# A transformer block on one core: score maxima planned up to three units ahead, their high parts from a second reduction, and the inverse steps in a new order

## The chip, the cores and the metric

The kernel runs on one core of a Trainium2 chip. The metric is the device time of one execution in microseconds; of several runs the median counts.

## The reference

A transformer block with conditioning. Two sequences of 2048 tokens, 512 wide, 16 heads of 32, all in float32:

```python
mod = silu(condition) @ Wada + bada
sh_a, sc_a, gt_a, sh_m, sc_m, gt_m = split(mod, 6, axis=1)
xm = layernorm(x, g1, be1) * (1 + sc_a) + sh_a
q, k, v = heads(xm @ Wqkv)
attn = softmax(where(causal, q @ k.T * 32**-0.5, -inf))
x = x + gt_a * ((attn @ v) @ Wproj + bproj)
xm = layernorm(x, g2, be2) * (1 + sc_m) + sh_m
x = x + gt_m * (gelu(xm @ W1 + b1) @ W2 + b2)
```

## The kernel before

The two sequences (`b`, called sequence 0 and 1 here; the class `Row` holds one) go one after the other through QKV, attention and projection; the MLP comes at the end for both. Attention is cut into 16 **units** per sequence, each a group of four heads (`c`, 0 to 3) and a block of 512 queries (`i`, 0 to 3). The order is i = 0, 1, 2, 3 for c = 0 and 0, 2, 1, 3 after it, so units 0, 4, 8, 12 have i = 0 and units 3, 7, 11, 15 have i = 3.

A query's exponentials need its maximum first, and the kernel gets the maxima by computing the scores twice:

- **The scores for the maxima**, queries on the partitions: one matmul into an `s` bank of PSUM (two banks; one in each step borrows an `st` bank) for each head, 128 queries and up to 512 keys (`bank`, L422). VectorE reduces each to one column of `mx`: L441, or L436 with the causal mask on the diagonal. When a unit is complete, `split` (L444) takes the maximum over the key blocks (L453, where there are several), writes it rounded to the matmul's fp32r type as the high part (L455) and the difference as the low part (L456), both into one of the `mhl` tiles. `rows` (L492) transposes that tile on TensorE (tile `ps_m`, in an `s` bank) and spreads it into `fold` on VectorE (L500).
- **The scores for the output**, keys on the partitions: a unit has 4i + 3 **steps**, one for each block of 128 keys with the last two of the diagonal put together. A step (`scores_t`, L524) starts with four `st<-fold` matmuls that put minus the maximum into the four `st` banks; then four heads' score matmuls add to them; ScalarE takes the exponential (L565, tile `e`); GpSimd zeroes what lies above the diagonal (L571). Two steps later TensorE multiplies with the values (tile `o`). For the sums of the exponentials (tile `sm`), GpSimd adds pairs and fours of steps first (L593, tile `ee`).

TensorE's matmuls stand in the order of the program, so the maxima's matmuls are put between those of the steps. A **planner** says how many: `due` (L645) finds the rate of VectorE work, in costs of `width + 190` or `width + 250`, that every later unit needs to be ready; `count` (L460) turns it into a number of scores `n` for this step, but takes none of a unit beyond `u + AHEAD`. `AHEAD` is 2 (L78): in unit 5, maxima of unit 7 may be computed, and none of unit 8. The queries of unit u + 3 are loaded at the start of unit u (L655) into one of AHEAD + 2 = 4 `qst` buffers; the keys of the next c at the start of its predecessor's first unit.

The sums of a unit go to DRAM (L619). Their **inverses** come back later: `load_sums` (L318) reads them spread over the partitions, `invert` (L328) takes the reciprocal on VectorE and stores it, `widen` (L332) copies it 32 times within DRAM, so that the projection can read it beside its operand. `inverses` (L341) places these by unit and step: the sums of units 0 to 11 in unit 12, step 2, their reciprocal in unit 13, step 0, their twelve widenings in pairs in steps 1 to 6 of unit 13; the sums of units 12, 13, 14 each in the next unit (step 6 of unit 13, step 2 of units 14 and 15), the reciprocal two steps later, the widening one after that. All these DMAs, the loads of queries and keys and the stores of outputs are issued from SP's one queue, in the order in which the builder of the program puts them. VectorE, too, works in order: what stands behind a waiting instruction waits.

Of the kernel before, what the change touches and what calls it, by code (L numbers as in the profile page):

```python
# [8 lines left out]
F32 = mybir.dt.float32  # L9
F32R = mybir.dt.float32r  # L10
BF16 = mybir.dt.bfloat16
AF = mybir.ActivationFunctionType
ALU = mybir.AluOpType
AX = mybir.AxisListType
# [3 lines left out]
P = 128  # L18
# [3 lines left out]
QB = 512  # L22
# [5 lines left out]
def dit_block_kernel(  # L28
# [35 lines left out]
    nc = tc.nc  # L64
# [5 lines left out]
    HC = P // HD  # L70
    TQ = QB // P
    NQ = T // QB
# [2 lines left out]
    LAG = 2  # L75
    E_BUFS = 12
    EE_BUFS = 12
    AHEAD = 2  # L78

    const = ctx.enter_context(tc.tile_pool(name="const", bufs=1))  # L80
    dram = ctx.enter_context(tc.tile_pool(name="scratch", bufs=1, space=DRAM))
# [1 line left out]
    def pool(name, bufs=1, **kw):  # L83
# [5 lines left out]
    bp = bp_cm.__enter__()  # L89
# [19 lines left out]
        axis=AX.XY,  # L109
        op=ALU.add,  # L110
# [7 lines left out]
    for n in range(AHEAD + 1):  # L118
        m = bp.tile([P, HC, HD], F32R, tag=f"mhl{n}", name=f"mhl{n}")
# [40 lines left out]
    n_early = (C - 1) * NQ  # L160
# [99 lines left out]
    units = []  # L260
# [4 lines left out]
    last_order = [i for _, i in units[-NQ:]]  # L265
# [8 lines left out]
    class Row:  # L274
# [30 lines left out]

        def load_queries(self, u):
            c, i = units[u]
            t = bp.tile([P, HC, QB], F32R, tag="qst", name="qst", bufs=AHEAD + 2)
            for r in range(4):
                nc.sync.dma_start(  # L310
                    t[r * HD : (r + 1) * HD].bitcast(F32),
                    qd[self.b][c][r // 2, :, i * QB : (i + 1) * QB].rearrange(
                        "(h d) t -> d h t", d=HD
                    ),
                )
            self.qst[u] = t

        def load_sums(self, u0, u1):  # L318

            w = (u1 - u0) * HC * QB // P  # L320
            self.r = bp.tile([P, n_early * HC * QB // P], F32, tag="r", name="r")[:, :w]
            nc.sync.dma_start(self.r, self.flat(sums_d, u0, u1))

        def flat(self, d, u0, u1):
# [15 lines left out]

        def inverses(self, u, n):  # L341

            if u < n_early:
                return
            if u == n_early:
                if n == 2:
                    self.load_sums(0, n_early)
                return
            if u == n_early + 1:
                if n == 0:  # L350
                    self.invert(0, n_early)
                elif n < 7:
                    for k in (2 * n - 2, 2 * n - 1):
                        self.widen(k)
                n -= 4
            if n == 2:
                self.load_sums(u - 1, u)
            elif n == 4:
                self.invert(u - 1, u)
            elif n == 5:  # L360
                self.widen(u - 1)

        def old_queries(self):

            t = bp.tile([P, HC, QB], F32R, tag="qst", name="qst", bufs=AHEAD + 2)
            return t.bitcast(F32)

        def prefetch(self):
# [75 lines left out]
        def split(self, u, mx):  # L444
            nb = units[u][1] + 1
            hl = mhl[u % (AHEAD + 1)][:, :, : 2 * TQ].rearrange(
                "p h (t l) -> p h t l", l=2
            )
            if nb == 1:
                m = mx[:, :, 0]  # L450
            else:
                m = bp.tile([P, HC * TQ], F32, tag="m1", name="m1", bufs=2)
                nc.vector.tensor_reduce(m, mx, axis=AX.X, op=ALU.max)  # L453
            m = m.rearrange("p (h t) -> p h t", h=HC)
            nc.vector.tensor_copy(hl[:, :, :, 0], m)  # L455
            nc.vector.tensor_tensor(  # L456
                hl[:, :, :, 1], m, hl[:, :, :, 0].bitcast(F32), ALU.subtract
            )
# [56 lines left out]
    def attention_phase(row):  # L515
        b, vv, kst, qst = row.b, row.vv, row.kst, row.qst
        with pool(f"att{b}") as ap, pool(
# [121 lines left out]
            for u, (c, i) in enumerate(units):  # L639
                for n, tiles in enumerate(steps_of[u]):  # L640
                    w = sum(QB - q for _, q in tiles)
# [3 lines left out]
            def due(u, step):  # L645

                rate, past = 0.0, weight[step]
                for v in range(u + 1, len(units)):

                    left = sum(weight[step : max(step + 1, starts[v] - 3)])  # L650
                    rate = max(rate, (cum[v] - row.spent) / left)
                return row.spent + rate * past

            for u, (c, i) in enumerate(units):
                if u + AHEAD + 1 < len(units) and u + AHEAD + 1 >= NQ:  # L655
                    row.load_queries(u + AHEAD + 1)
                if u % NQ == 0 and c + 1 < C:
                    row.load_keys(c + 1, 0, NG)
                steps = len(steps_of[u])
                for n_step, tiles in enumerate(steps_of[u]):  # L660
                    last = n_step == steps - 1
                    if n_step == 0:
                        summed, later = set(), []
                        o = ps_op.tile([P, QB], F32, tag="o", name="o")
                        sm = ps_op.tile([P, QB], F32, tag="sm", name="sm")
                    ready = row.at
                    n = row.count(
                        due(u, starts[u] + n_step) - QB // 2, u + AHEAD
                    )
                    es, rest = scores_t(u, n_step, n)  # L670
                    rest = len(row.todo) - rest
                    make_rows = False
                    if u + 1 < len(units) and row.rows_made == u + 1:
                        if last:
                            row.score(row.count(cum[-1], u + 1))
                        make_rows = last or (ready > u + 1 and n_step >= 1)
                    row.inverses(u, n_step)
                    if u == len(units) - 1:
                        row.prepare(n_step)
                    flush(now)  # L680
                    if make_rows:
                        row.rows(u + 1)
                    row.score(max(0, len(row.todo) - rest))

                    def tile_by_tile(dst, lhs, es, tiles, first, last):
                        at = 0
                        for n, (j, q) in enumerate(tiles):
                            products(
                                dst, lambda h: lhs(j, h), es, q, at,
                                first and n == 0, last and n == len(tiles) - 1,  # L690
                            )
                            at += QB - q

                    def values(es=es, tiles=tiles, c=c, o=o, first=n_step == 0, last=last):
                        tile_by_tile(
                            o,
                            lambda j, h: vv[:, j, (c * HC + h) * HD : (c * HC + h + 1) * HD],
                            es, tiles, first, last,
                        )

                    def row_sums(es, last, tiles=((0, 0),), sm=sm, summed=summed):
                        first = not summed
                        summed.add(len(summed))
                        tile_by_tile(sm, lambda j, h: ones[:, :HD], es, tiles, first, last)

                    if later:
                        four_sums(u, *later.pop(0))

                    pending.append((now + LAG, values))
                    if n_step >= i * TQ:  # L710
                        pending.append(
                            (
                                now + LAG,
                                lambda f=row_sums, es=es, tiles=tiles, last=last: f(
                                    es, last, tiles
                                ),
                            )
                        )
                    elif n_step % 2 == 0:
                        even = es  # L720
                    else:
                        ee = pair_sums(u, even, es)
                        if n_step % 4 == 1:
                            ee0 = ee
                        else:

                            end = n_step + 1 == i * TQ
                            for heads in ([(0, 1), (2, 3)] if end else [range(HC)]):
                                later.append((ee0, ee, heads))
                            pending.append(  # L730
                                (
                                    now + LAG + 2 + end,
                                    lambda f=row_sums, ee=ee0: f(ee, False),
                                )
                            )
                    if last:
                        pending.append((now + LAG, lambda u=u, o=o, sm=sm: finish(u, o, sm)))
                    pending.sort(key=lambda p: p[0])
                    now += 1
# [241 lines left out]
    row = Row(0)  # L981
# [492 lines left out]
```

## Time and profile before

| | |
|---|---|
| median of 3 runs | 2513.37 us (2510.52 to 2516.57) |
| the profiled execution | 2510.99 us, its span 2509.3 us, mean granted clock 0.99 |
| TensorE busy | 2440.3 us (97%) |
| VectorE busy | 1401.8 us (56%) |
| ScalarE busy | 892.6 us (36%) |
| GpSimd busy | 978.7 us (39%) |

The profile is one execution. Busy shares are means over phases that differ: the attention of sequence 0 lies at about 230 to 815 us, that of sequence 1 at 1062 to 1636 us, the MLP from 1699 us on. TensorE's busy time counts its pipelined matmuls with ends that are modelled, so that a stall of some tenths of a microsecond doesn't show in it; the spacing of the starts shows it. In a line of the trace, `tile<-tiles` names what is written and read, and the name after the arrow in brackets or behind a bar is what ended the idle time before it.

### The profile page before, as it was taken

Reading aid. Unit: us, or ns where it says so; the run is one execution under the profiler, and the core shown is the slowest. Engines: PE = TensorE matmul, PEld = TensorE weight load, DVE = VectorE, ACT = ScalarE, POOL = GpSimd, SP = SyncE. Lnnn points to the kernel's source line nnn. Section 1 sums busy time; section 2 is a strip of 40 time slices with the busy share of each in tenths; the row PEclk is TensorE's granted clock in tenths of the full one; section 3 lists DMA queues with packets and bytes.
Section 4 is the critical chain, followed back from the end, with each engine's and each line's share of the span. In section 5 each row is a group of like instructions: output and inputs, shape, how many; then the busy total and the mean of one; then the engine's idle time right before and its main releaser. Section 6 shows DMA issues by size and latency. Waiting matters only on the chain.

```text
span 2509.3 us, 30950 instructions
## 1 busy us (share of the span) xinstructions
PE 2440.3 (97%) x10977; PEld 1178.9 (47%) x10977; DVE 1401.8 (56%) x2820; ACT 892.6 (36%) x1667; POOL 978.7 (39%) x1158
## 2 busy tenths in 40 slices
PE   7999999999999999999999999999999999999998
PEld 3445545445444444554554454444444444444443
DVE  3455667767666535567676766664363353344424
ACT  1213555554545012155545454613313312311310
POOL 0052786766762361068667675332101101200200
PEclk9999999999999999999999999999999999999999
DMA  6667123051224695440514113263224233332423
GB/s 223 202 218 202 46 50 87 22 110 43 87 88 144 215 302 193 133 95 22 110 43 110 27 51 118 69 226 114 88 92 140 78 101 109 109 96 70 140 84 96
DMA packets 133445, 285.71 MB, mean 114 GB/s; under 512 B 13301, under 2 KB 42525, under 8 KB 128426
## 3 DMA queue, kind: packets, MB, share of 16 engines
q1 hardware_dynamic: 126226, 257.47, 34.4%
q0 software_dynamic: 5376, 23.07, 2.6%
q10 hardware_dynamic: 1688, 3.19, 0.4%
q8 instruction: 86, 1.41, 0.2%
q14 instruction: 69, 0.57, 0.1%
HBM read 209.76 MB, written 81.79 MB: 116 GB/s over the span
## 4 chain that ended last, share of the span: by engine, by line
PE 62%; DVE 3%; DMA 1%; SPq 1%; issue 1%; ACT 0%; DVEq 0%; ACTq 0%
PE ps_h L192 15%; PE ps_y L192 15%; PE st L192 9%; PE o L192 5%; PE s L192 5%; PE ps_qk L192 4%; PE ps_o L192 3%; PE sm L192 2%; PE ps_v L192 2%; SPq L336 1%; PE ps_xt L200 1%; PE ps_o L200 0%; DMA r<-sum 0%; DMA q<-hl 0%; DVE junk L436 0%
## 5 line engine op out<-in xcount | busy, mean ns | idle before, releaser
L565 ACT ACTIVATE e<-st 128x512 f32<-128x512 f32 (+1 forms) x1152 | 572.8, 579 | 516.7 <-PE st L192 458.0
L441 DVE TENSOR_REDUCE mx<-s 128x1 f32<-128x512 f32 x634 | 429.6, 687 | 236.2 <-PE s L192 233.4
L593 POOL TENSOR_TENSOR ee<-e 128x512 f32<-128x512 f32 x336 | 420.2, 1287 | 242.8 <-ACT e L565 242.8
L192 PE MATMUL s<-kst,qst 128*128 128x512 f32 (+3 forms) x1066 | 483.4, 460 | 28.4 <-DVE mx L441 10.4
L192 PE MATMUL st<-qst,kst 128*128 128x512 f32 (+3 forms) x1280 | 405.3, 393 | 0.0
L192 PE MATMUL o<-e,vv 128*32 128x512 f32 (+3 forms) x2560 | 296.5, 545 | 0.0
L192 PEld LDWEIGHTS s<-kst,qst 128*128 128x128 f32 x1066 | 201.3, 190 | 202.3 <-DVE mx L441 80.4
L192 PE MATMUL ps_h<-sx,w 128*128 128x512 f32 x640 | 286.7, 592 | 0.0
L1245 POOL TENSOR_TENSOR c<-c 128x512 f32<-128x512 f32 x32 | 40.6, 1270 | 626.8 <-DVE c L1207 626.8
L436 DVE CUSTOM_DVE_ANT_0 junk<-s,causal 128x384 bf16<-128x384 f32 (+3 forms) x432 | 212.2, 491 | 126.9 <-PE s L192 118.2
L192 PE MATMUL ps_y<-sh,w 128*128 128x512 f32 x640 | 276.7, 592 | 0.0
L192 PEld LDWEIGHTS st<-qst,kst 128*128 128x128 f32 x1280 | 226.9, 193 | 92.8 <-issue 63.2
L192 PE MATMUL ps_qk<-xmT,wqkv 128*128 128x512 f32 x512 | 242.0, 601 | 2.2 <-DVE xmT L248 2.2
L571 POOL TENSOR_SCALAR_AFFINE_SELECT e<-e 128x128 f32<-128x128 f32 (+1 forms) x384 | 122.8, 344 | 290.2 <-ACT e L565 284.2
L1207 DVE TENSOR_TENSOR h<-c,ps_h 128x512 f32<-128x512 f32 x128 | 88.0, 688 | 232.5 <-PE ps_h L192 232.5
L593 POOL TENSOR_TENSOR ee<-ee 128x512 f32<-128x512 f32 x168 | 211.2, 1285 | 0.0
L192 PEld LDWEIGHTS ps_h<-sx,w 128*128 128x128 f32 x640 | 121.1, 190 | 150.2 <-issue 149.7
L192 PEld LDWEIGHTS ps_y<-sh,w 128*128 128x128 f32 x640 | 120.7, 190 | 147.8 <-issue 146.4
L1231 ACT ACTIVATE h<-h,cols 128x512 f32<-128x512 f32 x128 | 92.3, 721 | 182.4 <-DVE h L1207 182.4
L192 PE MATMUL st<-fold,sel 32*128 32x512 f32 (+1 forms) x1152 | 154.0, 485 | 2.3 <-DVE fold L500 2.0
L192 PEld LDWEIGHTS ps_qk<-xmT,wqkv 128*128 128x128 f32 x512 | 95.2, 192 | 98.7 <-issue 91.2
L192 PEld LDWEIGHTS st<-fold,sel 32*128 32x128 f32 x1152 | 61.2, 183 | 145.3 <-ACT e L565 75.2
(123 smaller groups left out, 2361.8 us busy)
## 6 DMA issues: line engine op xcount, KB each, us to landing
qst<-q SPq DMA_DIRECT2D x128, 256.0 KB
w<-w1d SPq DMA_DIRECT2D x34, 896.0 KB
w<-w2d SPq DMA_DIRECT2D x28, 1024.0 KB
kst<-k SPq DMA_DIRECT2D x24, 1024.0 KB
q<-hl SPq DMA_DIRECT2D x32, 512.0 KB
k<-hl SPq DMA_DIRECT2D x32, 512.0 KB
kst<-k SPq DMA_DIRECT2D x32, 256.0 KB
w<-in_L_cond_W_dram POOLq DMA_DIRECT2D x64, 128.0 KB, 4.3
```

The lines of the kernel that those rows point to most:

```text
L192: return tc.keep_in_program_order(nc.tensor.matmul(*args, **kw))
L200: return tc.keep_in_program_order(nc.tensor.transpose(dst, src, ident[:n, :n]))
L336: nc.sync.dma_start(dst, inv_d[self.b][u].unsqueeze(1).to_broadcast([HC, HD, QB]),)
L436: nc.vector.tensor_tensor_reduce(junk[:, :w], s[:, :w], causal[:, QB - w :], 1.0, MASKED, ALU.add, ALU.max, m,)
L441: nc.vector.tensor_reduce(m, s[:, :w], axis=AX.X, op=ALU.max)
L565: act(nc.scalar.activation(e[:, :w], sts[h][:, :w], AF.Exp))
L571: nc.gpsimd.affine_select(d, d, pattern=[[0, len(tiles)], [1, P]], compare_op=ALU.is_ge, fill=0.0, base=0, channel_multiplier=-1,)
L593: act(engine.tensor_tensor(dst, x, y, ALU.add))
L1207: nc.vector.tensor_tensor(dst, x, y, op)
L1231: nc.scalar.activation(d, d, AF.Gelu, bias=col(r_b1 + chunk, 1))
L1245: nc.gpsimd.tensor_tensor(c1_, c1_, c2_, ALU.subtract)
```

## The change

Three things are changed. `AHEAD` becomes 3, with one exception in steps 0 and 1 of a unit, where the limit stays at u + 2. There is one more `mhl` tile (`AHEAD + 1` of them); the number of `qst` buffers is now `AHEAD + 1`, which is four again, and the queries of the same unit are loaded at the same place. The high part of the maxima is written by a second maximum over the key blocks instead of a copy of the first one's result. And the inverses are placed anew: the first reciprocal in unit 13, step 2, the first twelve widenings one in a step from step 3 of unit 13 on, in the order in which the projection reads them, the other sums loaded in step 3 and inverted and widened in step 6 of the next unit, with a tile of their own (`r1`).

```diff
-    AHEAD = 2
+    AHEAD = 3
...
-            t = bp.tile([P, HC, QB], F32R, tag="qst", name="qst", bufs=AHEAD + 2)
+            t = bp.tile([P, HC, QB], F32R, tag="qst", name="qst", bufs=AHEAD + 1)
...
             w = (u1 - u0) * HC * QB // P
-            self.r = bp.tile([P, n_early * HC * QB // P], F32, tag="r", name="r")[:, :w]
+            tag = "r" if u1 - u0 > 1 else "r1"
+            self.r = bp.tile([P, w], F32, tag=tag, name="r")
...
         def inverses(self, u, n):
-            if u < n_early:
+            k = u - n_early
+            if k < 0:
                 return
-            if u == n_early:
-                if n == 2:
-                    self.load_sums(0, n_early)
-                return
-            if u == n_early + 1:
-                if n == 0:
-                    self.invert(0, n_early)
-                elif n < 7:
-                    for k in (2 * n - 2, 2 * n - 1):
-                        self.widen(k)
-                n -= 4
-            if n == 2:
+            if (k, n) == (0, 2):
+                self.load_sums(0, n_early)
+            elif (k, n) == (1, 2):
+                self.invert(0, n_early)
+                self.early = sorted(
+                    range(n_early), key=lambda v: last_order.index(units[v][1])
+                )
+            elif k and (k > 1 or n > 2) and self.early:
+                self.widen(self.early.pop(0))
+            if k and n == 3:
                 self.load_sums(u - 1, u)
-            elif n == 4:
+            elif k and n == 6:
                 self.invert(u - 1, u)
-            elif n == 5:
                 self.widen(u - 1)
...
             m = m.rearrange("p (h t) -> p h t", h=HC)
-            nc.vector.tensor_copy(hl[:, :, :, 0], m)
+            nc.vector.tensor_reduce(
+                hl[:, :, :, 0],
+                mx.rearrange("p (h t) n -> p h t n", h=HC),
+                axis=AX.X,
+                op=ALU.max,
+            )
...
-                if u + AHEAD + 1 < len(units) and u + AHEAD + 1 >= NQ:
-                    row.load_queries(u + AHEAD + 1)
+                if NQ <= u + AHEAD < len(units):
+                    row.load_queries(u + AHEAD)
...
                     n = row.count(
-                        due(u, starts[u] + n_step) - QB // 2, u + AHEAD
+                        due(u, starts[u] + n_step) - QB // 2, u + AHEAD - (n_step < 2)
                     )
```

More of the change, by code (lines that the diff above doesn't have):

```diff
@@ L341, in inverses @@
         def inverses(self, u, n):
-            if u < n_early:
+            k = u - n_early
+            if k < 0:
                 return
-            if u == n_early:
-                if n == 2:
-                    self.load_sums(0, n_early)
-                return
-            if u == n_early + 1:
-                if n == 0:
-                    self.invert(0, n_early)
-                elif n < 7:
-                    for k in (2 * n - 2, 2 * n - 1):
-                        self.widen(k)
-                n -= 4
-            if n == 2:
+            if (k, n) == (0, 2):
[8 more added lines that the diff above has]
+            if k and n == 3:
                 self.load_sums(u - 1, u)
-            elif n == 4:
+            elif k and n == 6:
                 self.invert(u - 1, u)
-            elif n == 5:
                 self.widen(u - 1)
         def old_queries(self):
-            t = bp.tile([P, HC, QB], F32R, tag="qst", name="qst", bufs=AHEAD + 2)
+            t = bp.tile([P, HC, QB], F32R, tag="qst", name="qst", bufs=AHEAD + 1)
             return t.bitcast(F32)
```

## The prediction

> **What bounds the kernel now.** I read the page first: TensorE is busy in nearly every slice, VectorE in six or seven tenths of the two attention phases (slices 5 to 13 and 17 to 26), so what can be won is TensorE's short stalls there. The dearest VectorE row is the maxima, and its idle time is waiting for TensorE's score matmuls: the two pace each other.
>
> ```profile
> PE   7999999999999999999999999999999999999998
> DVE  3455667767666535567676766664363353344424
> L441 DVE TENSOR_REDUCE mx<-s 128x1 f32<-128x512 f32 x634 | 429.6, 687 | 236.2 <-PE s L192 233.4
> ```
>
> Next, the windows query on tile s over units 3, 4 and 5 of sequence 1, unit 3 cut in two: the stretch, its length, busy time and instructions of TensorE, weight loads and VectorE, clock, DMA.
>
> ```profile
> 1142.75:1181.82 39.07, 13.90 (x36) 6.81 (x36) 21.23 (x36) 1.00 0.12 30
> 1181.82:1197.50 15.68, 0.78 (x2) 0.38 (x2) 1.44 (x3) 1.00 0.03 9
> 1197.50:1213.29 15.79, 5.46 (x14) 2.61 (x14) 8.10 (x14) 1.00 1.03 218
> 1213.29:1259.40 46.11, 18.34 (x48) 8.85 (x48) 28.48 (x48) 1.00 0.34 77
> ```
>
> The score matmuls come unevenly: two in the last five steps of unit 3, then fourteen in the three steps of unit 4. (Where a step has three or more, one goes into an st bank, which this query leaves out.) Stepping L645 to L668 through with the planner's own costs gives exactly the number of score matmuls that the TensorE timeline shows in every one of 144 steps, so I trust it for the changed limit too.
>
> A step runs from its first st<-fold matmul to the next step's. Against it I set a floor: its matmuls at the start-to-start spacing that their kind has where nothing waits (a 512-wide score 0.22 us). What exceeds the floor in sequence 1, by scores in the step:
>
> | scores | steps | excess, us |
> |---|---|---|
> | 0 | 33 | 7.4 |
> | 2, 3 | 5 | 0.6 |
> | 4 | 26 | 7.5 |
> | 5 | 54 | 19.7 |
> | 6 | 23 | 28.1 |
> | 7 | 3 | 3.3 |
>
> Together 66.6 us, and 64.8 in sequence 0. The sixes hold 6.5 in one step that waits for a reciprocal, 13.6 in eight steps that also transpose maxima (1.2 to 2.8 each), 3.4 in one step at half clock, and 0.36 in each of the other thirteen. How such a step stalls (unit 6, step 4):
>
> ```profile
> 1277.60 0.56 DVE L455 CAST mhl<-m 128x16 fp32r<-128x16 f32 x1
> 1278.20 1.19 DVE L456 TENSOR_TENSOR mhl<-m,mhl 128x16 fp32r<-128x16 f32 x1
> ...
> 1279.65 0.49 PE L192 MATMUL s<-kst,qst 128*128 128x512 f32 x1 [1.04 <-DVE mx L436]
> ...
> 1282.52 0.39 PE L192 MATMUL s<-kst,qst 128*128 128x256 f32 x1 [0.41 <-DVE fold L500]
> ```
>
> VectorE is held up in the split, two s banks are full, TensorE waits in order. The reciprocal's stall, unit 13:
>
> ```profile
> 1522.48 20.22 SPq L336 DMA_DIRECT2D wide<-inv  x10
> 1542.75 2.41 SPq L322 DMA_DIRECT2D r<-sum  x1
> ...
> 1553.90 0.25 DVE L329 RECIPROCAL r<-r 128x16 f32<-128x16 f32 x1 [3.69 <-DMA r<-sum]
> ...
> 1554.76 0.80 PE L192 MATMUL s<-kst,qst 128*128 128x512 f32 x1 [3.11 <-DVE mx L441]
> ```
>
> The 8 KB of sums queue behind ten widenings of 256 KB and land 11.1 us after their issue.
>
> **What the Trainium skill says.** "SBUF — State Buffer", Who interferes with whom: a cast can take the port pair that VectorE shares with GpSimd, a tensor_tensor with both inputs in SBUF contends with GpSimd's reads, and a tensor_reduce on this chip never contends. The trace agrees on the kinds: the 24 reductions at L453 take 0.18 to 0.22 us, while the casts reach 7.39.
>
> ```profile
> L455 DVE CAST mhl<-m 128x16 fp32r<-128x16 f32 x24 | 50.9, 2119 | 0.5
> L456 DVE TENSOR_TENSOR mhl<-m,mhl 128x16 fp32r<-128x16 f32 x24 | 13.5, 560 | 0.6
> 1330.62 9.97 POOL L593 TENSOR_TENSOR ee<-e 128x512 f32<-128x512 f32 x8
> 1333.35 7.30 DVE L455 CAST mhl<-m 128x16 fp32r<-128x16 f32 x1
> ```
>
> This cast outlasted six GpSimd additions of 1.29 us, so it isn't just the one in progress that holds it. "DMA: Bandwidth & Descriptors", Queues, rings and completion order: descriptors are consumed in ring order, which fits the 11.1 us. "TensorE: Matmul & The Clock Gate", What's actually happening: after an idle window the clock halves. The window 1550.71 to 1560.85 has a granted clock of 0.66; a stall costs more than itself.
>
> **The change part by part.** *AHEAD 3.* The same units' queries are loaded at the same place (u + 3 before and after) into four buffers as before; only the planner's limit moves, by one unit, from step 2 on. Stepped again, a sequence has 20 steps with no score, 15 with three, 50 with four, 55 with five, 4 with six. TensorE's work is the same; the excess changes. No score: the two opening steps keep 1.6, 18 at 0.15 make 2.7. Three: unit 0's keeps its 2.2, 14 at 0.2 (the only one now shows 0.12) make 2.8. Four: 50 at 0.18 (plain ones now show 0.11 to 0.36) make 9.0. Five: 55 at 0.36 (19.7 over 54) make 19.8. Six: 1.4. Sum 39.5. The transposing steps now hold four or five scores; such ones show an extra 0 to 0.1 now, so 11 give 1.1, and two right behind a split get half of the 2.65 seen, 2.6. That is 43.2.
>
> *Second maximum.* It takes out 32 casts (24 at 2.12, 8 at 0.17: 52 us of VectorE) and adds 32 reductions of about 0.2 (L453's rows), 6.4 us. On the path I count nothing for this alone: the six casts of 7.3 us lie where no scores are planned (TensorE ran on at 2.55 and 3.31 us a step). With AHEAD 3 that cover is gone, four or five scores stand in those steps, and the casts would cost some 5.5 each. The subtraction at L456 stays and still needs the pair. Bounds: 0.2 us when free, 7.3 if it is starved like the cast; its 24 durations reach 1.50, so I take one GpSimd addition at most, and 0.3 us of TensorE for each of 13 splits: 3.9. A sequence is then at 47.1.
>
> *Inverses.* Same eight-kilobyte loads, reciprocals (0.25, the early one 1.34) and stores, same widenings, all on SP. The sums' load now stands behind one widening of unit 13 instead of ten, in a buffer of its own, and the reciprocal comes three steps later, 11 us or more. The 6.5 is therefore in none of my new sums. Behind the reciprocal on VectorE stand the maxima, behind the inverse's store on SP the later widenings; their reader, the projection's operands, comes a unit later. The first reciprocal moves two steps too. A fourth zeroed mhl tile costs 0.17 us before TensorE's first matmul, hidden by the first loads.
>
> Sum: 66.6 + 64.8 − 2 × 47.1 = 37.2. Projection, QKV and MLP phases: nothing. The profiled execution took 2510.99 (span 2509.3), 2.4 under the median 2513.37; so 2474 for such an execution and **2476 us** for the median.
>
> **The rivals.** *Starved subtraction (slower).* At AHEAD 3 the maxima follow each split at once; if GpSimd's additions (busy throughout 1181.82 to 1197.50) keep the subtraction out like the casts, 26 splits cost 7.3 less the 1.8 that two free s banks cover (scores come 0.9 us apart): 26 × 5.5 = 143, hence 2619. It decides from 37 / 26 = 1.4 us a split. Against it: the waits of 1.50 at most, though they always came behind a cast. If only the six at the old places starve, 33 are lost: 2509, no change. *Late queries.* In units 4, 8, 12 scores three ahead start at step 2, two steps of 4.1 us and 1.7 more after their 1 MB was issued (1195.74 in unit 4); at the 204 to 245 GB/s of the windows behind it that takes about 5 us. If they come 3 us too late: 6 × 3 = 18, hence 2494. *Not as it says.* DMA order is the builder's; if the load still lands behind the widenings, 12 us stay: 2488.
>
> **How the numbers follow.** Levelling 0.73, late queries or unmoved load 0.12, six starved or all gains eaten 0.05, starved 0.10. About 0.2%, 5 us, can be told from no change. The likeliest case alone is 2463 to 2490; the range reaches to the six starved, **2462 to 2509**. Faster 0.85, same 0.05, slower 0.10.
>
> **What would show it.** Right: s matmuls in every step of units 3, 7, 11; steps of four at 3.4 to 3.5 us, of five at 3.7 to 3.8; none of 5.8 or 6.1; no wait of L329; reductions at 0.2. Wrong: L456's successor above 2 us, score matmuls waiting for qst's DMA, or TensorE's excess still above 55 us a sequence.

## The result and the profile after

The changed kernel takes **2501.84 us** (median of 6 runs, 2499.7 to 2507.36) against 2515.81 of the kernel before (6 runs, 2510.52 to 2521.73). The medians lie 14 us apart; the ratio given for them is 0.9959 [0.9941, 0.9977], which is 10 us (6 to 15), and the spans of the profiled executions, 2509.3 before and 2499.4 after, lie 9.9 apart. The forecast was 2476. The sign is right and the time lies inside the range, but the gain is between a quarter and two fifths of the 37 us forecast.

The page first. The rows of TensorE and VectorE hardly change, and the dearest VectorE row has the same mean. It counts 28 fewer because as many more of its kind now lie in an `st` bank: more steps have three scores or more.

```profile
PE   7999999999999899999999999999999999999998
DVE  3455766766665635667666776574263353344424
L443 DVE TENSOR_REDUCE mx<-s 128x1 f32<-128x512 f32 x606 | 408.4, 687 | 221.4 <-PE s L192 220.8
```

One slice of TensorE (number 14) has dropped to 8, but it lies at 812 to 875 us, behind the attention of sequence 0, which ends at about 800; in before the same slice is busy for 91% and in after for 90%. It has no part in what follows. Below are the windows on tile `s` of after, at its own borders: unit 3 of sequence 1 cut in two at step 10, then units 4 and 5. The columns are those of the windows shown in the prediction.

```profile
1144.27:1182.58 38.31, 12.69 (x34) 6.39 (x34) 19.77 (x34) 1.00 0.13 31
1182.58:1208.19 25.61, 7.11 (x18) 3.42 (x18) 10.41 (x19) 0.93 0.04 7
1208.19:1221.24 13.05, 3.75 (x9) 1.70 (x9) 5.55 (x9) 1.00 1.00 217
1221.24:1263.36 42.12, 14.81 (x38) 7.14 (x38) 23.19 (x38) 1.00 0.42 95
```

The scores are spread as forecast: 18 `s` matmuls where there were 2, and unit 4 with 9 instead of 14. Unit 4 is shorter by 2.7 us and unit 5 by 4.0. But the last five steps of unit 3 take 25.6 us, 9.9 more than before. Sixteen more scores at 0.22 us are 3.5 us; the rest comes of a wait. The timeline of after shows which, first VectorE and GpSimd, then one line of TensorE (other lines left out):

```profile
1178.74 5.03 POOL L601 TENSOR_TENSOR ee<-ee 128x512 f32<-128x512 f32 x4
1182.79 0.20 DVE L455 TENSOR_REDUCE m<-mx 128x16 f32<-128x48 f32 x1
1182.91 0.19 DVE L458 TENSOR_REDUCE mhl<-mx 128x16 fp32r<-128x48 f32 x1
1183.14 5.57 DVE L464 TENSOR_TENSOR mhl<-m,mhl 128x16 fp32r<-128x16 f32 x1
1183.70 4.97 POOL L601 TENSOR_TENSOR ee<-e 128x512 f32<-128x512 f32 x4
1188.63 0.68 DVE L443 TENSOR_REDUCE mx<-s 128x1 f32<-128x512 f32 x1
...
1189.36 0.48 PE L192 MATMUL s<-kst,qst 128*128 128x256 f32 x1 [4.58 <-DVE mx L443]
```

GpSimd adds without a gap from 1178.74 to 1188.67. Both reductions of the split take 0.2 us. The subtraction (L456 before, L464 now) takes 5.57 us, and it ends at 1188.71, just when that run of additions (L593 before, L601 now) ends. Only then can VectorE reduce the next `s` bank, and TensorE, which had filled both banks and stopped, goes on after 4.58 us. In the window 1187 to 1192 the granted clock is 0.75, so the matmuls behind it pay too: step 10 of the unit takes 9.8 us; before, with two scores, it took 3.0, and in `pool_lo` below, with the same five scores as here, 3.7.

The kinds of the subtraction in after, from the groups by form (busy us, mean ns):

```profile
L464 DVE TENSOR_TENSOR mhl<-m,mhl 128x16 fp32r<-128x16 f32 x24 | 40.4, 1684 | 0.5
L464 DVE TENSOR_TENSOR mhl<-mx,mhl 128x16 fp32r<-128x16 f32 x8 | 9.3, 1165 | 0.2
```

Before, its first form took 13.5 us in all and the cast 50.9. The cast is gone and the subtraction has inherited the wait. The long ones stand in the splits of units 5, 9 and 13, made in units 3, 7 and 11 (5.55, 5.33, 4.17 in sequence 0 and 5.57, 5.30, 4.18 in sequence 1), and in that of unit 3 in sequence 0 (4.97); three of about 2.44 are in splits of units with i = 0. Each of these ten ends within 0.05 us of the end of a run of GpSimd's additions; in the three of 2.44 the run ends with maskings (L579, 0.3 us each). The list of waits names what TensorE waited for, first before, then after (us in all, times, longest):

```profile
PE s L192 <- DVE mx L441: 10.4, 9, 3.2
...
PE s L192 <- DVE mx L443: 24.4, 7, 4.6
...
PE s L192 <- DVE mx L438: 4.2, 2, 4.0
```

The reciprocal of the sums (L329 before, L330 now) no longer waits in unit 13, and that unit takes 41.4 us instead of 52.2, in both sequences.

### The profile page after: what moved, and what is told of

Its sections match the earlier page's. It is cut to its first block, busy times and chain, and to the rows that moved or that the text cites. A ratio compares the mean times of both kernels' runs of the same rounds, so it can differ in the third digit from the quotient of the medians.

```text
span 2499.4 us, 30991 instructions
## 1 busy us (share of the span) xinstructions
PE 2428.3 (97%) x10977; PEld 1178.4 (47%) x10977; DVE 1388.0 (56%) x2821; ACT 894.9 (36%) x1667; POOL 980.3 (39%) x1158
## 4 chain that ended last, share of the span: by engine, by line
PE 62%; DVE 3%; DMA 1%; issue 1%; ACT 0%; SPq 0%; DVEq 0%; ACTq 0%
PE ps_h L192 15%; PE ps_y L192 15%; PE st L192 10%; PE o L192 5%; PE s L192 5%; PE ps_qk L192 4%; PE ps_o L192 3%; PE sm L192 2%; PE ps_v L192 2%; PE ps_xt L200 1%; DVE mhl L464 1%; PE ps_o L200 0%; DMA q<-hl 0%; DVE mx L443 0%; DVE stat L204 0%
## 5 line engine op out<-in xcount | busy, mean ns | idle before, releaser
L443 DVE TENSOR_REDUCE mx<-s 128x1 f32<-128x512 f32 x606 | 408.4, 687 | 221.4 <-PE s L192 220.8
L601 POOL TENSOR_TENSOR ee<-e 128x512 f32<-128x512 f32 x336 | 420.3, 1289 | 242.7 <-ACT e L573 242.7
L192 PE MATMUL s<-kst,qst 128*128 128x512 f32 (+3 forms) x1032 | 469.7, 457 | 29.0 <-DVE mx L443 24.4
L192 PE MATMUL st<-qst,kst 128*128 128x512 f32 (+3 forms) x1280 | 414.4, 391 | 0.0
L438 DVE CUSTOM_DVE_ANT_0 junk<-s,causal 128x512 bf16<-128x512 f32 (+3 forms) x426 | 209.1, 491 | 156.4 <-PE s L192 148.7
L579 POOL TENSOR_SCALAR_AFFINE_SELECT e<-e 128x128 f32<-128x128 f32 (+1 forms) x384 | 123.3, 345 | 283.4 <-ACT e L573 280.7
L601 POOL TENSOR_TENSOR ee<-ee 128x512 f32<-128x512 f32 x168 | 211.5, 1289 | 0.0
```

The costliest lines, as they stand in the source:

```text
L192: return tc.keep_in_program_order(nc.tensor.matmul(*args, **kw))
L438: nc.vector.tensor_tensor_reduce(junk[:, :w], s[:, :w], causal[:, QB - w :], 1.0, MASKED, ALU.add, ALU.max, m,)
L443: nc.vector.tensor_reduce(m, s[:, :w], axis=AX.X, op=ALU.max)
L579: nc.gpsimd.affine_select(d, d, pattern=[[0, len(tiles)], [1, P]], compare_op=ALU.is_ge, fill=0.0, base=0, channel_multiplier=-1,)
L601: act(engine.tensor_tensor(dst, x, y, ALU.add))
```

## The experiments

Two theories were put against each other. **Held subtraction:** the levelling works as forecast, and a subtraction with both inputs in SBUF, waiting for GpSimd, gives most of it back. **Levelling worth little:** the steps of five scores cost what the sixes did, and the waits lie where TensorE would have stood anyway. All times below are medians, and each ratio is to the kernel before, with its 95% interval.

### The subtraction taken away from the contention

`psum_lo`: after, with the first maximum written into an `s` bank of PSUM, so that the subtraction has one input in SBUF. The eight splits with a single key block, which needed no first maximum, get one too.

```diff
-            if nb == 1:
-                m = mx[:, :, 0]
-            else:
-                m = bp.tile([P, HC * TQ], F32, tag="m1", name="m1", bufs=2)
-                nc.vector.tensor_reduce(m, mx, axis=AX.X, op=ALU.max)
+            m = ps_sp.tile([P, QB], F32, tag="s", name="m1")[:, : HC * TQ]
+            nc.vector.tensor_reduce(m, mx, axis=AX.X, op=ALU.max)
```

> The changed kernel, but the maximum m goes to an s bank of PSUM, so that the subtraction has one SBUF input. If the subtraction's waits behind GpSimd's additions ate the levelling (some 49 us over its eight longest places), this lands at about 2450 to 2456 and the subtraction takes under 0.4 us everywhere. If the levelling itself brings no more than the 10 us seen, it stays at 2497 to 2503, with the subtraction short or not.

`pool_lo`: after, with the subtraction on GpSimd.

```diff
-            nc.vector.tensor_tensor(
-                hl[:, :, :, 1], m, hl[:, :, :, 0].bitcast(F32), ALU.subtract
+            act(
+                nc.gpsimd.tensor_tensor(
+                    hl[:, :, :, 1], m, hl[:, :, :, 0].bitcast(F32), ALU.subtract
+                )
             )
```

> The changed kernel with the subtraction on GpSimd, in GpSimd's own order, so that VectorE never waits for the pair. Starved subtraction: 2452 to 2465, a little above the version with m in PSUM, since the transposition that follows a split closely now waits for GpSimd's queue. Levelling without worth: about 2500. GpSimd already the bound: above 2505.

Measured: `psum_lo` **2458.67** (0.9789 [0.9771, 0.9807]), `pool_lo` **2450.26** (0.9756 [0.9737, 0.9774]). Both take away nearly all that was lost, in two different ways. Tile `mhl` in `psum_lo` (ns: least, median, longest) and in `pool_lo`:

```profile
L461 DVE TENSOR_TENSOR mhl<-m,mhl x32: 165/174/178, 117.9 to 1529.6; 128x16 fp32r<-128x16 f32 x32
```

```profile
L465 POOL TENSOR_TENSOR mhl<-m,mhl x24: 216/223/264, 180.2 to 1522.7; 128x16 fp32r<-128x16 f32 x24
```

With one operand in PSUM all 32 take under 0.18 us, beside the same additions on GpSimd. The windows on tile `s` of `pool_lo` for the same stretches of unit 3 (its times are earlier, its work the same):

```profile
1114.69:1152.90 38.21, 12.71 (x34) 6.38 (x34) 19.65 (x34) 1.00 0.12 30
1153.01:1172.25 19.24, 6.64 (x18) 3.32 (x18) 10.43 (x19) 1.00 0.04 10
```

The first ten steps are as in after; the last five take 19.24 us instead of 25.61, at a full clock, which is the 15.7 of before and the 3.5 of the sixteen scores. This is the held subtraction's price in one place. `pool_lo` has no wait of an `s` matmul for VectorE among its eight largest on TensorE; `psum_lo`, whose maximum takes a turn in the two `s` banks, has 13 short ones (5.8 us), which is most of the 8 us between the two.

### Is it the second maximum?

`ahead3_copy`: after, with the copy for the high part, as before.

```diff
-            nc.vector.tensor_reduce(
-                hl[:, :, :, 0],
-                mx.rearrange("p (h t) n -> p h t n", h=HC),
-                axis=AX.X,
-                op=ALU.max,
-            )
+            nc.vector.tensor_copy(hl[:, :, :, 0], m)
```

> The changed kernel with the copy in place of the second maximum: three units ahead and new inverses, casts as before. If either instruction that needs the pair is held through the burst, the cast takes the wait and the subtraction behind it is short: 2495 to 2512, like the changed kernel. If the cast is the worse of the two and the second maximum was what kept it from being slow: above 2520.

Measured: 2500.09 (0.9956 [0.9939, 0.9973]), the same as after. The cast takes the wait again; its groups by form:

```profile
L457 DVE CAST mhl<-m 128x16 fp32r<-128x16 f32 x24 | 35.7, 1488 | 0.7
L457 DVE CAST mhl<-mx 128x16 fp32r<-128x16 f32 x8 | 10.9, 1366 | 0.1
```

The subtraction behind it has a median of 0.18 us and at most 1.22. So of the two instructions, the first takes the long waits, and the second follows free or nearly so. Taking the first out only moves the wait.

`before_reduce`: before, with the second maximum alone (the same edit in the other direction).

> The kernel before with the second maximum alone. If the subtraction takes over the wait of the cast, and the long casts lay under no scores: within 4 us of the kernel before, the subtraction at 4 to 7 us in units 3, 7, 11. If the cast's wait was on the path: 10 us faster or more.

Measured: 2501.71 (0.9952 [0.9933, 0.9971]), 12 us under before (7 to 17). The forecast gave this part nothing. The long waits stay, now in the subtraction (7.2 to 7.7 us), where no scores are planned. The profiled executions show 8.0 us of gain in units 6 and 10, where the wait of cast and subtraction had stood among the steps of six scores: all four take 30.4 us, where three took 31.6 and one 34.6. Of the 34.6, 2.8 us lie in one step at about half clock behind that wait (6.91 us for 4.11), which the other three don't have; so about 5 of the 8.0 come back in all four alike, 1.2 in each. Unit 2 of sequence 1 loses 4.1 us by a subtraction held 4.4; unit 0 of the two sequences gains 2.9, and what remains lies outside the attention, so at most the 8.0 are explained, and the rest of the 12 stays open.

`pool_lo_copyhi`: `pool_lo` with the copy for the high part.

> Three units ahead, new inverses, subtraction on GpSimd, but the high part by the copy on VectorE again. If copy and subtraction are held alike, and the second maximum is worth something only when the subtraction is off VectorE too, the copy is held at the same places for 4 to 6 us and the time is back at 2490 to 2503. If the subtraction alone was the trouble: 2450 to 2458.

Measured: 2459.96 (0.9784 [0.9765, 0.9803]), 10 us above `pool_lo`, and far from the 40 to 50 that a held cast would cost. Its longest cast takes 3.11 us, not 5.7. GpSimd's own subtraction needs the cast's result, and the additions behind it in the program come only after it. Each of the seven casts of over 0.4 us ends within 0.04 us of the end of the last addition in front of it, and the subtraction starts 0.1 us later (for one of 3.11: cast done at 1441.67, subtraction from 1441.75, next addition from 1441.93). The upper expectation left this out.

### The inverses

`before_inv`: before, with the new inverses alone. `pool_lo_oldinv`: `pool_lo` with the old ones. The edit is the hunk of `inverses` and of the tile `r1` in the change's diff, forwards and backwards.

> The kernel before with the new inverses alone. The wait for the sums (about 6.5 us of TensorE in each sequence) goes: 12 to 13 us faster. If the load only lands behind other transfers, or another wait follows: under 4 us.

> The version with the subtraction on GpSimd, with the old inverse steps. If the new inverses are worth what unit 13 showed in the profile of that part alone (5.4 us a sequence), this is 10 to 13 us above that version's 2450: 2460 to 2463. If the wait for the sums was worth only the 3 us that the part alone gained: 2452 to 2455.

Measured: `before_inv` 2507.86 (0.9984 [0.9973, 0.9995]), 4 us under before (1 to 7), where I expected 12. Its profile has unit 13 shorter by 5.4 us in both sequences, as expected, but in that execution the cast of one split in unit 2 was held 4.6 us in both sequences, and that unit was 4 to 5 us longer. `pool_lo_oldinv` 2474.42 (0.9842 [0.9823, 0.9861]), **24 us above** `pool_lo` by the medians and 22 by the ratios, where 10 to 13 were expected. Waits of VectorE, then of TensorE, in it:

```profile
DVE r L329 <- DMA r<-sum: 23.0, 6, 9.2
...
PE s L192 <- DVE mx L441: 16.2, 2, 8.2
```

The same late load that cost one wait of about 4 us a sequence at `AHEAD` 2 costs up to 9.2 at `AHEAD` 3, where the units are shorter and scores stand in every step; unit 13 takes 51.05 and 54.34 us against 41.4.

### The same parts at AHEAD 2

`before_pool`: before, with the second maximum and with the subtraction on GpSimd. `before_pool_inv`: the same with the new inverses. Against `pool_lo`, the second leaves out only `AHEAD` 3, with its fourth `mhl` tile and the exception in steps 0 and 1.

> The kernel before, two units ahead and old inverses, with high parts by the second maximum and the subtraction on GpSimd: VectorE never needs the pair in a split. If the long casts of before lay under no scores, only what stalls in units 2, 6 and 10 can go, 2 to 4 us a sequence: 3 to 9 us faster. If they mattered as they do three units ahead: 30 us faster or more.

> Two units ahead, second maximum, subtraction on GpSimd, new inverses. If the new inverses are worth 5 us a sequence at this limit, the time is 2492 to 2495, and the distance to 2450 (some 43 us) is what three units ahead give when VectorE isn't held. If the part is worth its 3 us here too: about 2500, and three units ahead give 50.

Measured: `before_pool` 2503.66 (0.9959 [0.9944, 0.9975]); `before_pool_inv` 2495.05 (0.9918 [0.9898, 0.9939]). The steps are then: the second maximum and the free splits 10 us (6 to 14), the new inverses 8.6 more (2503.66 to 2495.05), `AHEAD` 3 another 45 (2495.05 to 2450.26). The last two are differences of medians from different series, so good to a few us; by the ratios they are 10 and 41. The levelling is the large part, as forecast; it pays only when nothing holds VectorE at a split: after, which adds `AHEAD` 3 and the new inverses to `before_reduce` and leaves the subtraction on VectorE, takes 2501.84 where that one takes 2501.71.

### How long GpSimd holds it

In after the subtraction waits for the rest of one addition and up to four more of 1.29 us in a row. Two kernels tried to make a gap: `spacer` puts a memset of 128x1 behind each addition on GpSimd, `spacer_wide` a memset of 128x256 behind every second. What the memsets write is not used; everything else is after.

```diff
                 act(engine.tensor_tensor(dst, x, y, ALU.add))
+                if engine is nc.gpsimd and h % 2:
+                    gap = ap.tile([P, 256], F32, tag="gap", name="gap", bufs=2)
+                    act(nc.gpsimd.memset(gap, 0.0))
```

> The changed kernel with a GpSimd memset of one column behind each of its additions; it reads no SBUF, and nothing uses what it writes. If VectorE is kept out as long as GpSimd's reads follow one another and gets the pair in the gap, the subtraction waits 1.4 us at most and the time is 2452 to 2470 (GpSimd has some 50 us more to do). If a gap of this kind gives nothing away, the waits stay at 4 to 6 us and the time at 2495 or above.

> The changed kernel with a GpSimd memset of 256 columns behind every second addition, about 0.3 us that read no SBUF; nothing uses what it writes. If a longer gap in GpSimd's reads lets VectorE in, the subtraction waits 2.7 us at most and the time falls below 2475. If VectorE is held until GpSimd has nothing left to do, the waits stay at 4 us and more and the time at 2490 or above.

Measured: `spacer` 2494.85 (0.9911 [0.9882, 0.9939]), `spacer_wide` **2471.05** (two runs; 0.9828 [0.9803, 0.9853]). The timeline of `spacer` (only GpSimd and the subtraction):

```profile
1323.90 0.12 POOL L604 MEMSET gap<- 128x1 f32 x1
1323.96 1.31 POOL L601 TENSOR_TENSOR ee<-ee 128x512 f32<-128x512 f32 x1
1324.23 6.11 DVE L464 TENSOR_TENSOR mhl<-m,mhl 128x16 fp32r<-128x16 f32 x1
1325.19 0.12 POOL L604 MEMSET gap<- 128x1 f32 x1
1325.25 1.29 POOL L601 TENSOR_TENSOR ee<-e 128x512 f32<-128x512 f32 x1
```

The next addition starts 0.06 us after its memset, before the memset ends, so this was no real gap, and the subtraction was held through five of them, to the end of the run. Its longest holds here are 6.48 us, longer than in after. In tile `mhl` of `spacer_wide`:

```profile
L464 DVE TENSOR_TENSOR mhl<-m,mhl x24: 164/177/2657, 166.9 to 1539.1; 128x16 fp32r<-128x16 f32 x24
L464 DVE TENSOR_TENSOR mhl<-mx,mhl x8: 164/2194/2930, 117.9 to 1405.9; 128x16 fp32r<-128x16 f32 x8
```

Its memsets take 0.31 us, and no subtraction waits longer than 2.93 us, a little over two additions. All nine waits of over 1 us end within 0.05 us of the end of an addition that has a memset behind it. GpSimd has more work than in after (1041.0 us busy against 980.3), and the kernel is 31 us faster. That speaks for the pauses in GpSimd's reads, and against GpSimd's load as such.

## Why the prediction was right and wrong

**Right: the levelling.** Every step has the number of scores that the stepping gave. In `pool_lo`, where no split is held, the plain steps of four (one key block, eight value matmuls, no sums or transposition) take 3.37 to 3.50 us in all 60 cases and those of five 3.64 to 3.93; none of 5.8 or 6.1 is left. In after they are the same except where a held split stands. No score matmul waits for queries. The forecast's excess over the floor, without the splits' 3.9, was 43.2 us a sequence; `pool_lo`, in which the splits are free, has 42.0 and 43.7.

**Wrong: "I take one GpSimd addition at most, and 0.3 us of TensorE for each of 13 splits: 3.9."** This is the step that failed. It rested on 24 durations of the subtraction that reach 1.50 us (1.20 within the attention), all of them behind a cast, which at the six long places had already sat out the run of additions; the text of the rival said so and it was still counted as evidence. The better number stood beside it, the cast's 7.39. What the splits cost is the length of the attention in after less that in `pool_lo`: 570.7 − 539.4 = 31.3 us in sequence 0, 560.4 − 540.8 = 19.6 in sequence 1 (first to last step, from the starts of the `st<-fold` matmuls). That is 50.9 us instead of 7.8, and it matches the spans, 2499.4 − 2448.4 = 51.0. Both of the forecast's own signs for it came: ten subtractions above 2 us, and an excess of 67 us a sequence where it named 55.

The bookkeeping of the sum, in us for both sequences (excess over the floor, before 131.4):

| term | forecast | measured | from |
|---|---|---|---|
| levelling and inverses | 45.0 | 45.6 | excess of `pool_lo` 85.8 |
| splits | −7.8 | −48.8 | excess of after 134.6 less 85.8 |
| the floor | 0 | 11.1 | lengths of the attention less excess |
| other phases | 0 | 2.0 | span less attention |
| sum | 37.2 | 9.9 | spans |

The rows are good to some 2 us: after and `pool_lo` have the same matmuls of TensorE in the same order, and still the rule's floors differ by 2.1, which is why the splits show 48.8 here and 50.9 by length. The third row is a second, smaller miss: the forecast took the floor as constant, "TensorE's work is the same". The same rule gives 5.3 and 5.8 us less in after. A reading that no run isolates: in before 160 score matmuls follow straight on one of values, sums or transposition, in `pool_lo` 118, and the next matmul starts 0.43 us (median) after such a score of 512 keys, 0.23 after the others. That is an estimate of 42 × 0.2, some 8 of the 11 us. The table doesn't part the levelling from the inverses; the pair `pool_lo_oldinv` and `pool_lo` does, with 24 us for the inverses against the 13 that the forecast removed (6.5 a sequence), so at `AHEAD` 3 the stall would have grown.

**"On the path I count nothing for this alone" (the second maximum).** Wrong at `AHEAD` 2, of which it was said: 12 us, of which units 6 and 10 show 8 in the profiled executions. At `AHEAD` 3, where the forecast let the second maximum save a cast of some 5.5 us in the splits, it saved nothing: `ahead3_copy` and after are alike. The size of that cast was right (its longest 5.69), but the wait wasn't the cast's own.

**The rivals.** What came was the starved subtraction, in its smaller form, held at the six old places (in units 3, 7 and 11), once more in unit 2 of sequence 0, and for shorter times elsewhere. The forecast gave the six 0.05 and 33 us. Their steps 10 to 12 take 40 us longer in after than in `pool_lo`, 6.7 a place where the rival reckoned 5.5, although the subtraction was held only 5.0 on average and not 7.3: the clock falls behind the wait (0.75 and 0.53 in the two windows named here). The whole cost 51. By the rival's own point of decision, 37 / 26 = 1.4 us a split, 50.9 / 26 = 2.0 should have ended slower than before. It didn't because the gain that was there to be eaten, 45 in the forecast's sum, was too low: with free splits it is 61 (spans 2509.3 and 2448.4). Late queries and unmoved loads didn't occur. So that the total stayed within the range is in part luck: errors of opposite sign met, 41.0 us too little for the cost of the splits and 13.1 too little for the gain of the floor and the other phases. The range had also been drawn out to 2509 for the case of six starved splits, which is most of what came.

**The Trainium skill.** "SBUF — State Buffer", Who interferes with whom, names the mechanism, and the runs agree with three of its statements: reductions never contend (all of the split's in after, 0.16 to 0.22 us), a VectorE instruction with one SBUF input outside the 2-port modes doesn't (`psum_lo`, 0.18 at most), and of GpSimd's instructions those count that read SBUF (in `spacer_wide` the waits end where a memset follows). It describes the pair as taken "for the whole instruction"; here VectorE was kept out through runs of up to six additions of 1.29 us, which the forecast had seen for the cast and did not carry over. The measurement decides.

**What stays open.** Some waits end at the first border between two additions (1.19 us, unit 6 before), others only with the run. The records on GpSimd are too rough in their ends to say what differs, and no run tells these two apart.

## What to carry to other kernels

When a chain of two instructions contends for the same thing, the short duration of the second is no measure of it: the first has waited for both. Before removing the first, ask what the second will cost in its place, and price it like the first. Work planned into an empty stretch loses the cover that made a wait there free, so take the wait away with the same change: here by one operand in PSUM, or by moving 16 columns to GpSimd, which costs 0.22 us apiece and brings the kernel with the whole change to 2450.26 us.

## What the hardware showed beyond expectation

- A VectorE subtraction of 16 columns was held for 5.57 us by GpSimd additions that take 1.29 us each; a 0.12 us memset between the additions left it held (up to 6.48), a 0.31 us one after every two cut it to 2.93 or less.
- A wait of TensorE costs more than itself. In unit 7 of sequence 1 it waits 4.31 us until 1335.77; in the 5 us from 1336 its granted clock is 0.53. Step 10 there takes 9.3 us, and step 11, in which no matmul waits for VectorE, 6.3; in `pool_lo` the same steps take 3.7 and 4.3.
- The four runs each of `psum_lo` and `pool_lo` lie within 1.5 and 3.4 us, the 29 of the kernel before within 15. Held splits don't explain this by themselves: the four of `before_reduce`, held up to 7.7 us, lie within 1.9, and the four of `before_pool_inv`, held nowhere, within 8.0. What spreads the runs stays open.
